# Attention heads worked off in halves of 256 queries, with the next head's projections spread over the head's tiles

## The chip, the cores and the metric

The kernel runs on one core of a Trainium2 chip. A core has five engines with a queue each: TensorE (PE in the profile; its weight loads are listed as PEld), VectorE (DVE), ScalarE (ACT), GpSimd (POOL) and SyncE (SP), which here only issues DMA transfers. Matmul results land in PSUM, in banks of 128 x 512 floats; all else works in SBUF. The metric is the device time of one execution in microseconds (us). It is taken in several runs, and one further execution is recorded by the hardware profiler.

## The reference

Two sequences of 1024 tokens, 256 wide, go through four residual layers, each of them x + f(layernorm(x)), all in float32:

```python
x = x + _L0_attn_ref(_layernorm(x, axis=-1), ...)   # 16 heads of 128, causal, ALiBi
x = x + _L0_ffn_ref(_layernorm(x, axis=-1), ...)    # ternary weights, SiLU-gated, RMS norm
x = x + _L1_attn_ref(_layernorm(x, axis=-1), ...)   # state space (Mamba): conv, scan over tokens
x = x + _L1_ffn_ref(_layernorm(x, axis=-1), ...)    # gated, keeps the two largest of each four
```

The change is in the first of them. A head's share is this, with wq, wk, wv of 256 x 128 and wo of 128 x 256:

```python
q, k, v = xn @ wq, xn @ wk, xn @ wv
s = clip(q @ k.T / sqrt(128), -1024, 1024) + causal_mask + slope[h] * position_of_key
out += softmax(s) @ v @ wo
```

## The kernel before

**Chunks.** The tokens are cut into four chunks of 512: both halves (u = 0 and 1) of the first sequence, then of the second. A chunk goes through all four layers. The kernel writes two streams of work that run beside each other: the attention of chunk k, and `rest(k - 1)`, the three later layers of the chunk before it. Chunk 0's attention has instead the quantization of the ternary weights beside it. The last chunk's `rest(3)` runs alone at the end, with the output projections of chunk 2's last layer held back for it (`held`, `fill_in`).

**One head.** `attention()` (L382) goes over 64 heads, 16 a chunk, and over four tiles of 128 queries in each. For a tile, `scores` (L355) multiplies the tile's queries with all keys up to the tile's end. That is up to 512 keys in chunks with u = 0, and 640 to 1024 with u = 1, in pieces of 512. VectorE takes each piece out of PSUM with the clip and the causal mask (L366), adds the ALiBi row and finds the row's extreme in one pass (L372), and ScalarE takes the exponential and its row sum (L377). `turn` (L286) transposes the tile on TensorE in blocks of 128 and copies the blocks to pT (L296). `values` (L298) multiplies pT with v for all 512 queries of the head, in one PSUM bank, and copies the result to z (L309). `project` (L311) multiplies z with wo, and VectorE scales by the reciprocal of the row sums and adds to x (L324). `qkv` (L328) makes q, k and v of the next head.

**What sets the order.** `attention()` is a generator that yields after each tile. What is to come later stands in the list `later` with a number of tiles to wait. A tile's `turn` comes LAG = 2 tiles after its scores; `values` with the last turn, which is in the next head's tile 1; `project` one tile after that; `qkv` in tile 1. At a chunk's last tile the list is emptied at once. The loops at L970 to L978 draw one tile of attention, and then as many pieces of `rest` as its share of a list of costs (`cost`, L952) says, over the 64 tiles of a chunk. A piece of the state-space loop is one of 64 products: two multiplications on GpSimd (L736, L771), a scan on VectorE (L757), an exponential on ScalarE (L750), and four transposes that add on TensorE (L701). Its rows bs and cs are fetched by SP's queue (L691).

The order written is a priority, not the order issued. The framework's planner estimates when each instruction could start, takes the earliest written of those that can, chooses between VectorE and ScalarE for a copy written as `nc.any`, and fixes each engine's queue. Within a queue the chip keeps that order.

**Buffers that the change touches.** Names with one tag share a fixed number of buffers: pT three (a head with u = 0 holds one, with u = 1 two), z, kT, v and qT two, s four. PSUM has two banks for scores, three (`mm`) that serve pt, z, o and the projections of q, k and v, and three for the rest. `load_head` (L262) fetches the next head's weights and ALiBi row, and in chunks with u = 1 also the kept keys and values of the sequence's first half (L282, L283), which `qkv` stored in DRAM (L350, L352).

## Time and profile before

| | |
|---|---|
| Median of 3 runs | 1837.7 us (1834.47 to 1837.82) |
| Profiled execution, span from first to last instruction | 1836.9 us |
| What lies around that span | the page gives no other time for that execution; the median is 0.8 us above the span |
| TensorE, VectorE, ScalarE, GpSimd busy | 94%, 66%, 52%, 45% of the span |
| Matmul instructions, weight loads | 7956 of each |
| Mean granted TensorE clock | 0.989 |
| Attention of chunks 0, 1, 2, 3 (first L372 to the next chunk's) | 20 to 231, 231 to 735, 735 to 1123, 1123 to 1594 us |
| State-space loops beside chunks 1, 2, 3 | 355 to 566, 830 to 1005, 1244 to 1454 us |
| `rest(3)` alone | from 1594 us on |

In the profile a row names line, engine, operation and tiles as out<-in, then the shape. A matrix product in float32 is two matmul instructions with a weight load each, so that 64 heads with 4 or 8 products of z make 768. A matmul's time has the pipeline's depth in it, and in a stream the next one starts before it ends; the distance between starts is what it costs. A wait names the engine that stood, what it was about to do, and what it waited for.

### The profile page before, as it was taken

To read this page: it belongs to the slowest core of one execution; us is meant where nothing else is said; L and a number is where in the kernel's file an instruction comes from. 1 tells how busy PE (TensorE), PEld (TensorE's weight loads), DVE (VectorE), ACT (ScalarE), POOL (GpSimd) and SP (SyncE) were. 2 spreads that over 40 slices of the span, in tenths; PEclk is the share of its full clock that TensorE was granted. 3 is DMA by queue.
4 is the path that set the end of the run, shared out by engine and by line. 5 is a ranking of instruction groups with operands and counts; after the bars stand their busy time and mean duration, and the time that the engine had idled before them with its cause. 6 is when DMAs were issued, how large, how long until landed. Compare 5 with 4: busy or idle time off the path is not lost. (4 is left out here: it accounts for less than half of the span.)

```text
span 1836.9 us, 24217 instructions
## 1 busy us (share of the span) xinstructions
PE 1718.3 (94%) x7956; PEld 1144.2 (62%) x7956; DVE 1218.3 (66%) x2349; ACT 963.7 (52%) x1789; POOL 832.2 (45%) x674
## 2 busy tenths in 40 slices
PE   7999999998999999998888999999999999998899
PEld 4666666555656557755555667756656565566895
DVE  5666555777785473458886565557788655667975
ACT  3444474656563553555554545566555446446742
POOL 3324032588892000419998000418898500035870
PEclk9999999999999999999999999999999999999999
DMA  6443512466662311337787324227665430212541
GB/s 201 128 142 128 193 46 88 149 203 204 216 202 91 103 52 48 125 109 232 245 247 224 116 71 141 82 67 228 226 214 184 142 115 26 75 53 86 178 136 57
DMA packets 178301, 255.99 MB, mean 139 GB/s; under 512 B 16240, under 2 KB 90992, under 8 KB 177152
## 3 DMA queue, kind: packets, MB, share of 16 engines
q1 hardware_dynamic: 176752, 241.61, 41.4%
q0 software_dynamic: 1152, 12.58, 1.9%
q8 instruction: 63, 1.03, 0.2%
q14 instruction: 62, 0.51, 0.1%
q10 hardware_dynamic: 272, 0.26, 0.0%
HBM read 232.04 MB, written 22.35 MB: 138 GB/s over the span
## 5 line engine op out<-in xcount | busy, mean ns | idle before, releaser
L771 POOL TENSOR_TENSOR hc<-hs,cs 128x512 f32<-128x512 f32 x256 | 362.1, 1428 | 10.8 <-DVE ss L366 3.1
L362 PE MATMUL s<-kT,qT 128*128 128x512 f32 (+3 forms) x768 | 302.7, 495 | 19.9 <-DVE ss L366 18.0
L377 ACT ACTIVATE ss<-ss,nm 128x128 f32<-128x128 f32 (+7 forms) x256 | 198.8, 776 | 183.5 <-DVE nm L372 174.1
L366 DVE SCALAR_TENSOR_TENSOR ss<-s,lower 128x512 f32<-128x512 f32 (+3 forms) x384 | 204.6, 549 | 121.0 <-PE s L362 119.4
L736 POOL TENSOR_TENSOR db<-du,bs 128x512 f32<-128x512 f32 x192 | 259.2, 1356 | 44.4 <-DVE hs L757 30.6
L304 PE MATMUL z<-pT,v 128*128 128x512 f32 (+3 forms) x768 | 264.5, 492 | 10.9 <-ACT pT L296 10.2
L372 DVE CUSTOM_DVE_ANT_0 ss<-ss,alibi 128x128 f32<-128x128 f32 (+7 forms) x256 | 241.3, 945 | 3.5
L750 ACT ACTIVATE da<-dl,a_neg 128x512 f32<-128x512 f32 x256 | 177.9, 698 | 115.6 <-DVE hs L757 90.6
L304 PEld LDWEIGHTS z<-pT,v 128*128 128x128 f32 x768 | 142.8, 190 | 145.1 <-issue 92.7
L296 ACT COPY pT<-pt 128x512 f32<-128x512 f32 (+3 forms) x321 | 145.4, 474 | 162.0 <-PE pt L293 160.4
L293 PE MATMUL pt<-ident,ss 128*128 128x128 f32 x1152 | 180.3, 279 | 32.1 <-DVE x L324 18.5
L293 PEld LDWEIGHTS pt<-ident,ss 128*128 128x128 f32 x1152 | 140.0, 142 | 94.7 <-DVE x L324 33.0
L362 PEld LDWEIGHTS s<-kT,qT 128*128 128x128 f32 x768 | 127.9, 193 | 84.1 <-issue 43.4
L757 DVE TENSOR_TENSOR_SCAN hs<-da,db 128x512 f32<-128x512 f32 x128 | 153.8, 1210 | 38.6 <-ACT da L750 20.8
L757 DVE TENSOR_TENSOR_SCAN hs<-da,carry,db 128x512 f32<-128x512 f32 x128 | 159.1, 1269 | 24.4 <-POOL hc L771 14.7
L324 DVE SCALAR_TENSOR_TENSOR x<-o,rr,x 128x256 f32<-128x256 f32 x256 | 108.9, 476 | 76.7 <-PE o L318 76.5
L701 PE MATMUL y<-ident,hc 128*128 128x128 f32 x1024 | 144.8, 279 | 8.4 <-POOL hc L771 8.4
L342 PEld LDWEIGHTS pv<-wv,xT_a 128*128 128x128 f32 x1024 | 124.4, 192 | 37.1 <-issue 25.3
L342 PE MATMUL pv<-wv,xT_a 128*128 128x128 f32 x1024 | 125.8, 275 | 5.5 <-ACT zs L309 3.4
L701 PEld LDWEIGHTS y<-ident,hc 128*128 128x128 f32 x1024 | 121.0, 145 | 14.3 <-POOL hc L771 11.9
L318 PE MATMUL o<-wo,zs 128*128 128x256 f32 x512 | 125.4, 386 | 4.1 <-ACT kT L338 3.0
L335 PE MATMUL pq<-xT_a,wq 128*128 128x512 f32 x256 | 122.7, 601 | 0.7 <-ACT xT_a L148 0.7
(204 smaller groups left out, 2468.7 us busy)
## 6 DMA issues: line engine op xcount, KB each, us to landing
cs<-bcd SPq DMA_DIRECT2D x256, 256.0 KB, 3.8
bs<-bcd SPq DMA_DIRECT2D x192, 256.0 KB, 4.3
alibi<-alibi_d SPq DMA_DIRECT2D x32, 512.0 KB, 4.2
wq<-in_wqT_dram SPq DMA_DIRECT2D x64, 128.0 KB, 3.5
wk<-in_wkT_dram SPq DMA_DIRECT2D x64, 128.0 KB, 3.1
wv<-in_wvT_dram SPq DMA_DIRECT2D x64, 128.0 KB, 2.8
wo<-in_woT_dram SPq DMA_DIRECT2D x64, 128.0 KB, 2.8
alibi<-alibi_d SPq DMA_DIRECT2D x32, 256.0 KB, 3.6
```

Of the source, the lines that this page charges most:

```text
L293: nc.tensor.transpose(tp[:, i, :], s[:, (kb0 + i) * P : (kb0 + i + 1) * P], ident)
L304: nc.tensor.matmul(zp[:, q0:], lhsT=st["v_all"][:, kb, :], rhs=st["pts"][kb // 4][:, kb % 4, q0:], start=(kb == 0), stop=(kb == last),)
L342: nc.tensor.matmul(vp[:, t, :], lhsT=xT[:, c, t * P : (t + 1) * P], rhs=st["v"][:, c, :], start=(c == 0), stop=(c == KC - 1),)
L362: nc.tensor.matmul(sp[:, :n], lhsT=st["qT"][:, j * P : (j + 1) * P], rhs=st["kT"][:, k0 : k0 + n], start=True, stop=True,)
L366: nc.vector.scalar_tensor_tensor(s[:, k0 : k0 + n], sp[:, :n], CLIP, lower[:, S - W + k0 : S - W + k0 + n], op0=ALU.min, op1=ALU.max,)
L372: pace["tile"] = nc.vector.tensor_tensor_reduce(out=s[:, :W], in0=s[:, :W], in1=st["alibi"][:, :W], scale=1.0, scalar=3.0e38, op0=ALU.add, ...
L377: nc.scalar.activation(s[:, :W], s[:, :W], AF.Exp, bias=nm, scale=-1.0, accum_out=st["rs"][:, j : j + 1])
L701: nc.tensor.matmul(yTs[c][:, t * P : (t + 1) * P], lhsT=h[:, t * P : (t + 1) * P], rhs=ident, is_transpose=True, start=start and t == 0, s ...
L736: nc.gpsimd.tensor_tensor(db[i], du, brow.pop(i), ALU.mult)
L750: nc.scalar.activation(da[i], parts[c][0], AF.Exp, scale=a_neg[:, c, n : n + 1])
L757: nc.vector.tensor_tensor_scan(out=hs[i], data0=da.pop(i), data1=db.pop(i), initial=0.0 if first else carry[:, n, c : c + 1], op0=ALU.mult ...
L771: nc.gpsimd.tensor_tensor(hc[i], hs.pop(i), crow.pop(i), ALU.mult)
```

## The change

A head's last steps are done for 256 queries at a time. `values` and `project` get a number `half`: z of a half goes over the keys up to that half's end, into the left half of a PSUM bank, and its copy, the reciprocal of its row sums and its two additions to x follow from it. z has three buffers of half the size. A half's `values` comes LAG + 1 = 3 tiles after the half's last scores, `project` one tile later. That puts them, for a head's first half, in the next head's tiles 0 and 1, and for the second half in tiles 2 and 3.

`qkv` is cut in three: `queries` in tile 0, `keys` in tile 1 and `new_values` in tile 3. The kept v is fetched in tile 2 (`load_values`), the kept k as before. The next chunk's layernorm is written in tile 2 of the last head but one (before: tile 0 of the last head).

At a chunk's end `later` is no longer emptied: its steps fall in the first four tiles of the next chunk. Only after the very last tile is it worked off, in the order of tiles. So `rest(k - 1)` begins with the chunk's fourth tile, and its costs are spread over 61 tiles.

```diff
--- before.py
+++ after.py
@@ -278,10 +278,13 @@
         w["kT"] = a2.tile([P, S], F32, tag="kT", name=f"kT_{k}_{h}")
         w["v_all"] = a2.tile([P, NT, DH], F32, tag="v", name=f"v_{k}_{h}")
         if u:
-            kd, vd = kept.pop((b, h))
-            nc.sync.dma_start(out=w["kT"][:, :U], in_=kd)
-            nc.sync.dma_start(out=w["v_all"][:, :UT, :], in_=vd)
+            nc.sync.dma_start(out=w["kT"][:, :U], in_=kept.pop(("k", b, h)))
         return w
+
+    def load_values(k, h, w):
+        b, u = CH[k]
+        if u:
+            nc.sync.dma_start(out=w["v_all"][:, :UT, :], in_=kept.pop(("v", b, h)))
 
     def turn(k, h, j, s, st):
 
@@ -295,47 +298,62 @@
                 )
             nc.any.tensor_copy(st["pts"][kb0 // 4][:, 0:n, j * P : (j + 1) * P], tp[:, 0:n, :])
 
-    def values(k, h, st):
+    def values(k, h, half, st):
         u = CH[k][1]
-        zp = ps_z(f"z_{k}_{h}")
-        last = (u + 1) * UT - 1
+        zp = ps_z(f"z_{k}_{h}_{half}")
+        at, W = half * UT // 2, U // 2
+        last = u * UT + at + UT // 2 - 1
         for kb in range(last + 1):
-            q0 = max(0, kb - u * UT) * P
+            q0 = max(0, kb - u * UT - at) * P
             nc.tensor.matmul(
-                zp[:, q0:], lhsT=st["v_all"][:, kb, :],
-                rhs=st["pts"][kb // 4][:, kb % 4, q0:], start=(kb == 0), stop=(kb == last),
+                zp[:, q0:W], lhsT=st["v_all"][:, kb, :],
+                rhs=st["pts"][kb // 4][:, kb % 4, at * P + q0 : at * P + W],
+                start=(kb == 0), stop=(kb == last),
             )
-        st["z"] = a2.tile([P, U], F32, tag="z", name=f"zs_{k}_{h}")
-        nc.any.tensor_copy(st["z"], zp)
-
-    def project(k, h, st):
-
-        rr = a3.tile([P, UT], F32, tag="rr", name=f"rr_{k}_{h}")
-        nc.vector.reciprocal(rr, st["rs"])
-        for t in range(0, UT, 2):
-            op = ps_mm(f"o_{k}_{h}_{t}").rearrange("p (a m) -> p a m", a=2)
-            for i in range(2):
-                ended["by"] = nc.tensor.matmul(
-                    op[:, i, :], lhsT=st["z"][:, (t + i) * P : (t + i + 1) * P], rhs=st["o"],
-                    start=True, stop=True,
-                )
-            for i in range(2):
-                xt = x[k][:, t + i, :]
-                nc.vector.scalar_tensor_tensor(
-                    xt, op[:, i, :], rr[:, t + i : t + i + 1], xt, op0=ALU.mult, op1=ALU.add
-                )
-
-    def qkv(k, h, st, xT):
-        u = CH[k][1]
+        st["z"][half] = a2.tile([P, W], F32, tag="z", name=f"zs_{k}_{h}_{half}", bufs=3)
+        nc.any.tensor_copy(st["z"][half], zp[:, :W])
+
+    def project(k, h, half, st):
+
+        at = half * UT // 2
+        rr = a3.tile([P, UT // 2], F32, tag="rr", name=f"rr_{k}_{h}_{half}")
+        nc.vector.reciprocal(rr, st["rs"][:, at : at + UT // 2])
+        op = ps_mm(f"o_{k}_{h}_{half}").rearrange("p (a m) -> p a m", a=2)
+        for i in range(2):
+            ended["by"] = nc.tensor.matmul(
+                op[:, i, :], lhsT=st["z"][half][:, i * P : (i + 1) * P], rhs=st["o"],
+                start=True, stop=True,
+            )
+        for i in range(2):
+            xt = x[k][:, at + i, :]
+            nc.vector.scalar_tensor_tensor(
+                xt, op[:, i, :], rr[:, i : i + 1], xt, op0=ALU.mult, op1=ALU.add
+            )
+
+    def turned_input(n, k, h, st, xT):
+        pp = ps_mm(f"p{n}_{k}_{h}")
+        for c in range(KC):
+            nc.tensor.matmul(
+                pp, lhsT=st[n][:, c, :], rhs=xT[:, c, :], start=(c == 0), stop=(c == KC - 1)
+            )
+        return pp
+
+    def queries(k, h, st, xT):
         st["qT"] = a2.tile([P, U], F32, tag="qT", name=f"qT_{k}_{h}")
+        nc.scalar.activation(
+            st["qT"], turned_input("q", k, h, st, xT), AF.Copy, scale=-1.0 / math.sqrt(DH)
+        )
+
+    def keys(k, h, st, xT):
+        b, u = CH[k]
         kT = st["kT"][:, u * U : (u + 1) * U]
-        for n, dst, scale in (("q", st["qT"], -1.0 / math.sqrt(DH)), ("k", kT, 1.0)):
-            pp = ps_mm(f"p{n}_{k}_{h}")
-            for c in range(KC):
-                nc.tensor.matmul(
-                    pp, lhsT=st[n][:, c, :], rhs=xT[:, c, :], start=(c == 0), stop=(c == KC - 1)
-                )
-            nc.scalar.activation(dst, pp, AF.Copy, scale=scale)
+        nc.scalar.activation(kT, turned_input("k", k, h, st, xT), AF.Copy, scale=1.0)
+        if u < NU - 1:
+            kept["k", b, h] = dr.tile([P, U], F32, tag="kd", name=f"kd_{k}_{h}", bufs=H)
+            nc.sync.dma_start(out=kept["k", b, h], in_=kT)
+
+    def new_values(k, h, st, xT):
+        b, u = CH[k]
         vp = ps_mm(f"pv_{k}_{h}").rearrange("p (t m) -> p t m", t=UT)
         for t in range(UT):
             for c in range(KC):
@@ -346,11 +364,8 @@
         v = st["v_all"][:, u * UT : (u + 1) * UT, :]
         nc.any.tensor_copy(v, vp)
         if u < NU - 1:
-            kd = dr.tile([P, U], F32, tag="kd", name=f"kd_{k}_{h}", bufs=H)
-            nc.sync.dma_start(out=kd, in_=kT)
-            vd = dr.tile([P, UT, DH], F32, tag="vd", name=f"vd_{k}_{h}", bufs=H)
-            nc.sync.dma_start(out=vd, in_=v)
-            kept[CH[k][0], h] = kd, vd
+            kept["v", b, h] = dr.tile([P, UT, DH], F32, tag="vd", name=f"vd_{k}_{h}", bufs=H)
+            nc.sync.dma_start(out=kept["v", b, h], in_=v)
 
     def scores(k, h, j, st):
 
@@ -385,38 +400,45 @@
         live = [load_head(0, 0)]
         for k in range(1, len(CH)):
             load_x(k)
-        qkv(0, 0, live[0], xns[0])
+        for f in (queries, keys, new_values):
+            f(0, 0, live[0], xns[0])
         later = []
         for i, (k, h) in enumerate(heads):
             st = live.pop(0)
-            if i + 1 < len(heads):
-                live.append(load_head(*heads[i + 1]))
+            ahead = heads[i + 1] if i + 1 < len(heads) else None
+            if ahead:
+                live.append(load_head(*ahead))
             u = CH[k][1]
             st["pts"] = [
                 a3.tile([P, 4, U], F32, tag="pT", name=f"pT_{k}_{h}_{i}") for i in range(u + 1)
             ]
             st["rs"] = a3.tile([P, UT], F32, tag="rs", name=f"rs_{k}_{h}")
+            st["z"] = {}
             for j in range(UT):
                 s = scores(k, h, j, st)
                 later.append((LAG, lambda a=(k, h, j, s, st): turn(*a)))
-                if j == UT - 1:
-                    later.append((LAG, lambda a=(k, h, st): values(*a)))
-                    later.append((LAG + 1, lambda a=(k, h, st): project(*a)))
-                if j == UT - 1 and h == H - 1:
-                    for _, f in later:
-                        f()
-                    later = []
-                else:
-                    now = [f for n, f in later if n == 0]
-                    later = [(n - 1, f) for n, f in later if n]
-                    for f in now:
-                        f()
-                if j == 1 and i + 1 < len(heads):
-                    qkv(*heads[i + 1], live[0], xns[heads[i + 1][0]])
-                if j == 0 and h == H - 1 and k + 1 < len(CH):
+                if j % 2:
+                    later.append((LAG + 1, lambda a=(k, h, j // 2, st): values(*a)))
+                    later.append((LAG + 2, lambda a=(k, h, j // 2, st): project(*a)))
+                now = [f for n, f in later if n == 0]
+                later = [(n - 1, f) for n, f in later if n]
+                for f in now:
+                    f()
+                if ahead:
+                    if j == UT // 2:
+                        load_values(*ahead, live[0])
+                    make = {0: queries, 1: keys, UT - 1: new_values}.get(j)
+                    if make:
+                        make(*ahead, live[0], xns[ahead[0]])
+                if j == UT // 2 and h == H - 2 and k + 1 < len(CH):
 
                     with tc.issue_after(tiles[-UT].ins) if k == 0 else nullcontext():
                         normed(k + 1)
+                if not ahead and j == UT - 1:
+                    while later:
+                        for f in [f for n, f in later if n == 0]:
+                            f()
+                        later = [(n - 1, f) for n, f in later if n]
                 yield k
 
 
@@ -971,8 +993,10 @@
         r, done = rest(k - 1), 0.0
         for i in range(H * UT):
             next(heads)
+            if i < UT - 1:
+                continue
             whole = cost(k - 1)
-            while done < whole * (i + 1) / (H * UT):
+            while done < whole * (i + 2 - UT) / (H * UT + 1 - UT):
                 done += next(r, whole)
         for _ in r:
             pass
```

## The prediction

> **What bounds the kernel now.** I read the page's first part, then stretches of the span cut where the state-space loop begins and ends, then TensorE's waits, then one head's matmuls in order of time, then the end of the last head.
>
> ```profile
> PE 1718.3 (94%) x7956; PEld 1144.2 (62%) x7956; DVE 1218.3 (66%) x2349; ACT 963.7 (52%) x1789; POOL 832.2 (45%) x674
> ```
>
> TensorE (PE) is the bound on average, but its busy time counts pipeline latency, so stages must be seen one by one (columns: PE, weight loads, DVE, ACT, POOL busy us, clock, DMA):
>
> ```profile
> 20.00:231.00 211.00, 204.91 (x968) 135.58 (x968) 139.88 (x390) 101.85 (x255) 58.33 (x51) 1.00 0.46 149
> 355.00:566.00 211.00, 192.63 (x941) 127.44 (x940) 170.12 (x298) 122.72 (x223) 184.68 (x132) 1.00 0.66 207
> 830.00:1005.00 175.00, 141.91 (x709) 101.13 (x710) 143.53 (x209) 93.09 (x194) 169.24 (x130) 0.93 0.78 240
> 1244.00:1454.00 210.00, 192.45 (x942) 127.53 (x941) 168.80 (x301) 122.99 (x223) 184.93 (x132) 1.00 0.65 209
> ```
>
> The first is chunk 0's attention, the others the state-space loops beside the attention of chunks 1, 2 and 3. In chunk 2 GpSimd (POOL) sets the pace: 169 of 175 us. In chunks 1 and 3 PE leaves 18 us of 211 and POOL 26.
>
> ```profile
> PE pt L293 <- DVE x L324: 18.5, 16, 2.4
> PE s L362 <- DVE ss L366: 18.0, 21, 1.3
> PE z L304 <- ACT pT L296: 10.2, 13, 1.7
> ...
> PE pt L293 <- ACT ss L377: 6.0, 8, 2.0
> ```
>
> These are the attention's own waits (us in total, times, longest). Their cause is in the order of one head of chunk 1:
>
> ```profile
> 426.95 5.86 PE L304 MATMUL z<-pT,v 128*128 128x512 f32 x16
> 432.64 1.88 PE L335 MATMUL pq<-xT_a,wq 128*128 128x512 f32 x4
> 434.36 1.88 PE L335 MATMUL pk<-xT_a,wk 128*128 128x512 f32 x4
> 436.08 1.95 PE L342 MATMUL pv<-wv,xT_a 128*128 128x128 f32 x16
> ...
> 439.37 1.89 PE L318 MATMUL o<-wo,zs 128*128 128x256 f32 x8
> 441.10 0.60 PE L293 MATMUL pt<-ident,ss 128*128 128x128 f32 x4
> ...
> 445.05 0.33 PE L293 MATMUL pt<-ident,ss 128*128 128x128 f32 x1 [1.62 <-DVE x L324]
> ...
> 451.74 1.56 PE L362 MATMUL s<-kT,qT 128*128 128x512 f32 x4 [1.25 <-DVE ss L366]
> ```
>
> From 426.95 to 437.86 PE does values and projections alone; no score is made, and VectorE (DVE) gets no tile. Then scores and transposes come faster than DVE empties their banks, and PE waits.
>
> **Spacings.** Starts a row apart divided by the count give what an instruction costs in a stream: 128x512 0.430 us (432.64 to 434.36, four), 128x256 0.216 (439.37 to 441.10, eight), projected values 0.111 (1.78 in 16), transposes 0.109 (same chunk: eight from 453.14 to 454.01); a 384-wide one I take as 0.323, between them. By these a head of chunks 1 and 3 costs PE 21.0 us: before, its four tiles take 1.8, 13.0, 3.8 and 2.4 us; after, 6.0, 4.8, 5.3 and 5.0. A head of chunks 0 and 2 costs 12.3 (2.2 scores, 2.2 z, 1.1 transposes, 1.7 o, 3.4 q and k, 1.8 v), 3.1 a tile.
>
> **Halved values: +1.** z has 768 instructions; halves make 32 x 6 x 2 + 32 x 14 x 2 = 1280, with 512 more weight loads. The columns are the same (1280 and 3328 a head): 10 x 0.430 + 2 x (0.323 + 0.216 + 0.109) = 5.60 us before, 24 x 0.216 + 4 x 0.109 = 5.62 after, under 1 us over 32 heads. The bound on the other side is every added load in the open: the row of z's loads has 190 ns, 512 x 0.190 = 97 us. I take the low end, because L318 is just such a stream, 256 wide with a load each, and runs at 0.216.
>
> The Trainium skill speaks against this edit: "TensorE: Matmul & The Clock Gate", section "The mechanism", lets a load overlap a running matmul only where the row groups differ, and its section "LDWEIGHTS (loading the stationary operand)" prices 128 columns at 128/1.2 = 107 ns. All loads here use all rows, so by that rule the 512 would add 55 us and the sum below would be about 1870. The trace disagrees: o's eight matmuls and eight loads fit in 1.73 us.
>
> **Twice as many small steps: +1.** 64 more reciprocals of 168 ns are 10.8 us of DVE. z's evictions become 128 of about 373 ns (the row of pT at 128x256 on ScalarE, ACT) for 64 of 581: 10.6 us more. ACT is 52% busy, and outside the two loops DVE idles; in the loops DVE is 170 of 211 and PE waits on it, 8 heads x 168 ns, 1.3 us each. I take 1; without cover it is 21.
>
> **Projections and values spread: -23.** The waits that uneven tiles make, by stretch: 8.5 (s on ss), 5.2 (pt on x), 2.2 (z on pT), 1.0 (pv on zs) in chunk 1's loop; 7.8, 4.9, 2.2, 1.0 in chunk 3's; 3.4 (pt on the exponential), 1.2, 0.7 in chunk 0: 38 us. Chunk 2's are left out, since POOL sets its pace. I take 60%: a loop that lost all its waits would take 194 us, not far from POOL's own work, 64 x 2 x 1.27 + 12 x 1.27 = 178, and two engines that near to each other's time still stop each other now and then. Ends: 38 gained, or nothing; below nothing is a rival. What is late next is POOL.
>
> **The rest starts three tiles later: +5.** L972's loop spreads the former chunk's later layers over 61 tiles, not 64. The state-space loop has 2.2 x 69 = 152 of 303 cost units in chunk 2, so it lies beside 30.6 tiles, not 32.1. It still takes POOL's 175 us, and 1.5 tiles x 3.1 us of attention fall outside: +4.6. In chunks 1 and 3 PE is the nearer bound and the same move costs nothing unless POOL takes over.
>
> **Chunks run on into each other: 0, and -5 at the end.** At the three inner boundaries PE's order already mixes the old chunk's values with the next scores; its waits there are at most 0.8 us each. After the last head nothing covers:
>
> ```profile
> 1596.55 1.09 PE L293 MATMUL pt<-ident,ss 128*128 128x128 f32 x8 [2.00 <-ACT ss L377]
> ...
> 1597.88 5.86 PE L304 MATMUL z<-pT,v 128*128 128x512 f32 x16 [0.24 <-ACT pT L296]
> ...
> 1604.41 1.99 PE L318 MATMUL o<-wo,zs 128*128 128x256 f32 x8 [0.68 <-ACT zs L309]
> 1605.58 1.74 DVE L324 SCALAR_TENSOR_TENSOR x<-o,rr,x 128x256 f32<-128x256 f32 x4 [7.21 <-PE o L318]
> ```
>
> Only the second half needs the last tile: 14 x 0.216 + 2 x 0.109 = 3.2 us of z, not 5.7 (-2.4), two x additions, not four (-0.9), and the first pair of layernorm tiles is out of the way (its xn starts 1.6 ahead of the second's, -1.6). The first half fills the 2.0 us of wait. Ends -2.4 and -7.
>
> **Moved at no cost.** The load of kept v (32 of them) goes two tiles later on SP's queue, and still waits there for the old buffer's last reader (SP stood 183.6 us, 18 times, at L283 for z). Behind it wait the bs and cs rows and the next weights. It lands in 3.6 us and is read over four tiles later. Without that cover POOL waits: all waits on bs make 13.8 us now. The stores of k and v are as many as before. Layernorm of the next chunk goes two tiles ahead, as does its first reader.
>
> **Sum.** 1836.9 (the profiled span) + 1 + 1 - 23 + 4.6 - 5 = 1815.5. The median of the runs shown is 0.8 above that span; so 1816.
>
> **Rivals.** *POOL takes the loops over* (chance 0.15). With 61 tiles the loops of chunks 1 and 3 hold 1.5 x 5.25 = 8 us less of PE's work, and PE's gain there is eaten: chunk 0 gives 3 and the end 5, against 7 of cost: 1836. For it: POOL 185 of 211. Against: its own work is 178, the rest its waits on DVE's scans (13.6 and 17.1 us).
>
> *A new wait at the second half of z* (0.25, slower). In chunks 1 and 3 a head holds two of the three pT buffers. The whole z was done 8 us before the next head's first transposes (432.6 to 441.1); its second half now stands in the same tile, just ahead of them. If the copy of the last pT is late there, PE stops, with scores, projections and the state space's transposes queued behind it, and ACT waits for a buffer. Such waits are there now: 13, mean 0.8, longest 1.7. One in each of 32 heads at 1.2 us is 38: 1854. It decides from 22 / 32 = 0.7 us a head. Against: the copy has a tile of 5 us to be done in.
>
> *Nothing spreads* (0.05). The order written is not the order issued: at 745 us z matmuls stand between layernorm's transposes. If the planner makes the same lumps, the sum without the 23 is 1839.
>
> My forecast has 0.55, with 1795 to 1832 as its own range. The range 1792 to 1850 leaves out a tenth on each side: a gain beyond all 38 of the waits, and the dearer half of the second rival. 0.2% (3.7 us) is about what a measurement of this kernel can tell from no change. Faster: 0.54 from the forecast, 0.06 and 0.02 from the first and third rivals; same 0.09; slower 0.25 and a few hundredths from the others.
>
> **What would show it.** Right: z x1280 with o's spacing of 0.216 kept; waits of s on ss and pt on x under half; chunk 1's and 3's loops near 200 us, chunk 2's still 175; the end of attention about 5 us shorter. Wrong: z's loads in the open, z's wait on pT at 32 times, or the loops still at 211 with POOL over 195.

## The result, and the profile after

The changed kernel takes 1857.3 us (median of 4 runs, 1855.36 to 1863.3) against 1837.8 in runs beside it: 1.0122 times the time, 95% interval 1.0102 to 1.0143. It is slower by 20 us, where 21 us less were forecast.

The profiled execution is the longest of the four (1863.3 us; its span is 1861.4), 6 us over the median. Busy time of the engines, whole span:

```profile
PE 1735.5 (93%) x8468; PEld 1249.4 (67%) x8468; DVE 1308.0 (70%) x2552; ACT 947.3 (51%) x1736; POOL 821.3 (44%) x674
```

The 512 added matmuls and loads are there. VectorE (DVE) is busy 90 us longer, ScalarE (ACT) 16 less: the planner put 72 of the 128 copies of z on DVE (12 of 64 before), and 137 copies of pT (63 before).

Busy time in stretches, as in the prediction (columns: window, length, PE, weight loads, DVE, ACT, POOL with counts, granted clock, DMA share, GB/s): chunk 0's attention, and the state-space loops beside chunks 1, 2 and 3.

```profile
20.00:220.00 200.00, 199.84 (x1031) 146.56 (x1030) 158.85 (x427) 98.17 (x254) 57.18 (x51) 1.00 0.48 156
360.00:580.00 220.00, 196.89 (x988) 145.17 (x987) 182.90 (x326) 109.07 (x195) 182.31 (x133) 0.94 0.62 195
847.00:1025.00 178.00, 139.02 (x710) 99.57 (x709) 150.77 (x221) 90.24 (x186) 167.16 (x130) 0.92 0.75 228
1275.00:1495.00 220.00, 197.37 (x988) 144.88 (x987) 182.02 (x326) 109.11 (x194) 182.34 (x133) 0.94 0.61 194
```

Chunk 0 has become 11 us shorter, and TensorE (PE) is busy in 199.8 of its 200 us. The loops take 220, 178 and 220 us, for 211, 175 and 210. POOL has a little less to do in them (182.3 us, for 184.7) and stands longer. The clock, 1.00 in loops 1 and 3 before, is 0.94.

PE's waits, whole span (us in total, times, longest):

```profile
PE pq L336 <- DVE zs L314: 25.5, 10, 4.4
PE y L723 <- POOL hc L793: 23.5, 22, 2.1
PE o L323 <- DVE zs L314: 10.5, 7, 2.4
...
PE z L308 <- ACT pT L299: 3.0, 3, 2.3
PE pt L296 <- DVE x L329: 2.7, 2, 1.7
PE s L377 <- DVE ss L381: 2.0, 2, 1.0
```

The waits that were to go are gone: s on ss 18.0 to 2.0 us, pt on x 18.5 to 2.7, z on pT 10.2 to 3.0. New ones stand first: the products pq and o now wait for z's copy, 43.6 us in all with two smaller rows. For o the copy is its input; q's projection needs a PSUM bank of the `mm` set, of which z holds one until it is copied.

**Where the time went.** I cut both traces at the reduction of each chunk's first tile of scores (L372 before, L387 after), at that of the very last tile, and at the first and last of a loop's 64 multiplications hc. PE's *work* in a part is its matmuls times the spacing of their width (0.430, 0.216, 0.109 us; about half of it for the ternary layer's products, of which 512-wide ones start 0.23 us apart at 1638 us after). *Idle* is the rest, so it holds PE's waits and also what a halved clock costs.

| Part | before | after | difference |
|---|---|---|---|
| up to the first tile | 19.5 | 20.3 | +0.8 |
| chunk 0 (idle in it) | 211.7 (14.5) | 199.4 (2.7) | -12.3 |
| chunks 1 to 3, outside the loops: duration (work, idle) | 766.3 (730.7, 35.5) | 784.2 (752.5, 31.7) | +17.9 |
| the three loops: duration (work, idle) | 596.5 (496.4, 100.2) | 617.5 (475.3, 142.2) | +20.9 |
| after the last tile | 242.9 | 240.0 | -2.9 |
| sum | 1836.9 | 1861.4 | +24.5 |

What is lost is PE's idle time in the loops, 42 us more, and it has two parts: the loops are 21 us longer, and 21 us of PE's work that lay in them now lies outside. The loops of chunks 1 and 3 hold 28 tiles of attention, for 31. In loop 1 PE's waits sum to 23 us, 18 before, and its halved clock costs up to 13.7, nothing before. By chunk the attention of chunks 1, 2 and 3 takes 6, 15 and 18 us longer.

**How a loop stands.** Three queues, each kept in order, wait on each other. In loop 1 (what each engine waited for; after, then before):

```profile
POOL db L758 <- DVE hs L779: 22.4, 3, 8.4
POOL hc L793 <- PE y L723: 9.1, 4, 4.1
DVE ss L381 <- PE s L377: 25.6, 10, 5.9
```

```profile
POOL db L736 <- DVE hs L757: 13.6, 3, 5.9
DVE v L347 <- PE pv L342: 15.9, 2, 8.0
DVE hs L757 <- ACT da L750: 10.4, 4, 9.4
DVE ss L366 <- PE s L362: 8.9, 11, 3.3
```

All of DVE's waits there sum to 34 us after and 41 before, so DVE does not stand longer, but elsewhere in its queue. POOL's sum to 37 and 26.

And one of after's three stands in order of time, from PE's, DVE's and POOL's timelines (start, us, idle before it in brackets):

```profile
414.86 0.87 DVE L387 CUSTOM_DVE_ANT_0 ss<-ss,alibi 128x640 f32<-128x640 f32 x1
...
420.32 1.02 DVE L381 SCALAR_TENSOR_TENSOR ss<-s,lower 128x512 f32<-128x512 f32 x2 [3.79 <-PE s L377]
421.38 1.79 DVE L387 CUSTOM_DVE_ANT_0 ss<-ss,alibi 128x768 f32<-128x768 f32 x1
...
426.23 0.69 DVE L381 SCALAR_TENSOR_TENSOR ss<-s,lower 128x512 f32<-128x512 f32 x1 [1.59 <-PE s L377]
...
427.90 1.21 DVE L779 TENSOR_TENSOR_SCAN hs<-da,db 128x512 f32<-128x512 f32 x1
```

```profile
418.63 3.72 POOL L793 TENSOR_TENSOR hc<-hs,cs 128x512 f32<-128x512 f32 x3 [0.55 <-PE y L723]
429.19 2.05 POOL L758 TENSOR_TENSOR db<-du,bs 128x512 f32<-128x512 f32 x1 [6.83 <-DVE hs L779]
```

From 413.8 to 427.9 DVE's queue holds no scan. It stands twice there for scores that PE makes late. POOL runs out of scans, needs the next one to free a buffer of db, and stands 6.83 us. PE in turn lacks POOL's products: its wait of y on hc, second in its list above, was 8.4 us before. The longest stretch without a scan in loops 1 and 3 is 10.1 us before and 16.1 after.

### The profile page after: what moved, and what is told of

Read it like the earlier page. It is cut to its first block, busy times and chain, and to the rows that moved or that the text cites. A ratio compares the mean times of both kernels' runs of the same rounds, so it can differ in the third digit from the quotient of the medians.

```text
span 1861.4 us, 25366 instructions
## 1 busy us (share of the span) xinstructions
PE 1735.5 (93%) x8468; PEld 1249.4 (67%) x8468; DVE 1308.0 (70%) x2552; ACT 947.3 (51%) x1736; POOL 821.3 (44%) x674
## 4 chain that ended last, share of the span: by engine, by line
PE 63%; DVE 11%; POOL 10%; issue 6%; DMA 5%; ACT 4%; SPq 1%; POOLq 0%; DVEq 0%; ACTq 0%
PE s L377 9%; PE z L308 8%; PE pq L336 5%; POOL hc L793 5%; PE pk L336 5%; PE pt L296 4%; PE o L323 4%; DVE hs L779 4%; PE pv L360 4%; POOL db L758 3%; PE g_g L463 3%; PE in L630 3%; PE u_g L463 3%; DMA cs<-bcd 3%; PE y L723 2%
## 5 line engine op out<-in xcount | busy, mean ns | idle before, releaser
L793 POOL TENSOR_TENSOR hc<-hs,cs 128x512 f32<-128x512 f32 x256 | 343.4, 1360 | 30.9 <-PE y L723 20.4
L758 POOL TENSOR_TENSOR db<-du,bs 128x512 f32<-128x512 f32 x192 | 267.1, 1400 | 67.2 <-DVE hs L779 44.8
L308 PE MATMUL z<-pT,v 128*128 128x256 f32 (+1 forms) x1280 | 274.0, 360 | 3.2 <-ACT pT L299 3.0
L308 PEld LDWEIGHTS z<-pT,v 128*128 128x128 f32 x1280 | 238.6, 191 | 49.3 <-ACT pT L299 4.9
L387 DVE CUSTOM_DVE_ANT_0 ss<-ss,alibi 128x128 f32<-128x128 f32 (+7 forms) x256 | 256.9, 1003 | 5.4
L299 ACT COPY pT<-pt 128x512 f32<-128x512 f32 (+3 forms) x247 | 115.8, 486 | 161.7 <-PE pt L296 160.7
L296 PE MATMUL pt<-ident,ss 128*128 128x128 f32 x1152 | 170.9, 275 | 2.7 <-DVE x L329 2.7
L336 PE MATMUL pq<-xT_a,wq 128*128 128x512 f32 x256 | 135.8, 654 | 31.9 <-DVE zs L314 25.5
L323 PE MATMUL o<-wo,zs 128*128 128x256 f32 x512 | 135.6, 385 | 13.3 <-DVE zs L314 10.5
L336 PE MATMUL pk<-xT_a,wk 128*128 128x512 f32 x256 | 127.1, 620 | 7.9 <-ACT qT L343 4.0
```

Source lines behind the costliest of these rows:

```text
L296: nc.tensor.transpose(tp[:, i, :], s[:, (kb0 + i) * P : (kb0 + i + 1) * P], ident)
L308: nc.tensor.matmul(zp[:, q0:W], lhsT=st["v_all"][:, kb, :], rhs=st["pts"][kb // 4][:, kb % 4, at * P + q0 : at * P + W], start=(kb == 0), ...
L323: ended["by"] = nc.tensor.matmul(op[:, i, :], lhsT=st["z"][half][:, i * P : (i + 1) * P], rhs=st["o"], start=True, stop=True,)
L336: nc.tensor.matmul(pp, lhsT=st[n][:, c, :], rhs=xT[:, c, :], start=(c == 0), stop=(c == KC - 1))
L387: pace["tile"] = nc.vector.tensor_tensor_reduce(out=s[:, :W], in0=s[:, :W], in1=st["alibi"][:, :W], scale=1.0, scalar=3.0e38, op0=ALU.add, ...
L758: nc.gpsimd.tensor_tensor(db[i], du, brow.pop(i), ALU.mult)
```

## The experiments

The recorded expectations number the theories in the order in which they came up. Those that matter: copies of z on VectorE hold PSUM banks, TensorE stands for them and its clock falls (1); the rest, crowded into 61 tiles, makes GpSimd the pace (2); the spread itself is at fault (3); GpSimd and the scans pace the loops, so late scans become lost time (4); the order that the planner writes is a draw, which any change of the program redraws (7); the even order is worse in itself (8).

### e1: is it the clock, or z's copies on VectorE?

```diff
-        nc.any.tensor_copy(st["z"][half], zp[:, :W])
+        nc.scalar.copy(st["z"][half], zp[:, :W])
```

> The changed kernel with one edit: the copy of z is tied to ScalarE. Theory 1 (the copies of the halves that fell to VectorE, 72 of 128, stand behind scans and hold a PSUM bank that the next query projection needs; TensorE stands up to 4.4 us there and its clock then falls): the waits of pq and o on zs (43.6 us now) fall under 10, the granted clock in the state-space loops of chunks 1 and 3 goes from 0.94 to 0.98 or more, these loops from 220 to about 205 us, and the time from 1857 to 1822 to 1835. Theory 2 (the rest of the former chunk, crowded into 61 tiles, makes GpSimd the pace): the loops stay at 215 or more, the waits move to another releaser, and the time stays over 1848.

Measured: 1864.0 us, 1.0148 (1.0122 to 1.0173). The loops, and the largest of PE's waits:

```profile
362.00:582.00 220.00, 192.18 (x989) 139.52 (x988) 179.72 (x315) 110.76 (x205) 183.47 (x133) 0.98 0.63 195
...
1278.00:1497.00 219.00, 192.08 (x986) 140.26 (x985) 179.27 (x315) 111.06 (x205) 181.77 (x132) 0.97 0.63 194
```

```profile
PE pq L336 <- ACT zs L314: 37.3, 14, 5.2
...
PE o L323 <- ACT zs L314: 6.3, 9, 1.2
```

The clock is back at 0.98 and 0.97 and the loops last as long as with 0.94: losing less clock did not shorten them. The waits for z's copy did not fall: they are 43.6 us as before the edit, now all on ACT. So the part of theory 1 that blames VectorE and the clock falls, but what these waits cost is not tested here. e4 below bears on it: it has no wait of pq on zs, and its loops are as long in sum.

### e2, e3, e4: the parts of the change one by one

e2: the changed kernel, with the list worked off at each chunk's last tile and the rest spread over 64 tiles again.

```diff
-                if not ahead and j == UT - 1:
+                if h == H - 1 and j == UT - 1:
...
-            if i < UT - 1:
-                continue
             whole = cost(k - 1)
-            while done < whole * (i + 2 - UT) / (H * UT + 1 - UT):
+            while done < whole * (i + 1) / (H * UT):
```

> The changed kernel without its last part: the list of later steps is worked off at each chunk's last tile, and the rest is spread over 64 tiles again. Theory 2 (61 tiles): the loops of chunks 1 and 3 go back to 31 tiles and about 211 us, chunk 2's outside part loses its 5 us, and the time falls to 1835 to 1843. Theory 1 (copies of z on VectorE): the waits on zs and the low clock in the loops stay, and the time stays at 1850 to 1860.

e3: the kernel before, with chunks that run on and the rest from the third tile.

```diff
-                if j == UT - 1 and h == H - 1:
...
+                if j == UT - 1 and i + 1 == len(heads):
...
+            if i < LAG:
+                continue
             whole = cost(k - 1)
-            while done < whole * (i + 1) / (H * UT):
+            while done < whole * (i + 1 - LAG) / (H * UT - LAG):
```

> The kernel before with the run-on alone: the list of later steps is not worked off at a chunk's end, and the rest begins with the chunk's third tile and is spread over 62. Theory 2: slower, 1843 to 1850, with the loops of chunks 1 and 3 over fewer than 31 tiles and POOL waiting no more. Theory 1: chunk 2 loses 3 to 5 us outside its loop as forecast, the loops of chunks 1 and 3 stay near 211 us at full clock, and the time is 1836 to 1842.

e4: the kernel before, with q, k and v of the next head made in tiles 0, 1 and 3 (and the next chunk's layernorm where the change has it).

```diff
...
-                if j == 1 and i + 1 < len(heads):
-                    qkv(*heads[i + 1], live[0], xns[heads[i + 1][0]])
+                if i + 1 < len(heads):
+                    make = {0: queries, 1: keys, UT - 1: new_values}.get(j)
+                    if make:
+                        make(*heads[i + 1], live[0], xns[heads[i + 1][0]])
...
```

> The kernel before with the spread of the projections alone: queries in tile 0, keys in tile 1, values in tile 3, z whole. Theory 1 (halved z on VectorE is the cause): no wait of pq on zs comes up, the waits of s on ss and pt on x fall by half, and the time is 1822 to 1835. Theory 3 (the spread itself is at fault: a projection in each tile asks for one of the three shared PSUM banks while they wait for copies): new waits of pq, pk or pv of 20 us or more, clock below 0.98 in the loops, and 1845 to 1855.

Measured: e2 1849.6 us, 1.0059 (1.0035 to 1.0083); e3 1886.9, 1.0273 (1.0255 to 1.0290); e4 1853.0, 1.0086 (1.0067 to 1.0105). Spread alone costs 14 us, run-on alone 48, halves with spread 11, and all three together 20: the parts do not add. e2 lies between the ranges of its two theories and e3 above both of its own; e4 lies in theory 3's range, but without the new waits of projections that theory 3 asked for. By part of the span:

| Kernel | chunk 0 | three loops | PE's work in them | idle in them |
|---|---|---|---|---|
| before | 211.7 | 596.5 | 496.4 | 100.2 |
| e4, spread alone | 203.3 | 618.8 | 497.7 | 121.2 |
| e2, without run-on | 201.6 | 627.8 | 496.2 | 131.6 |
| e3, run-on alone | 211.1 | 601.8 | 467.4 | 134.4 |
| after | 199.4 | 617.5 | 475.3 | 142.2 |

Chunk 0, which has no scans beside it, gains 8 us from the spread and a few more from the halves. In e4 PE's wait of s on ss is gone (18.0 us before), but pt on x stays at 17.2 us and z on pT grows from 10.2 to 27.4: the spread alone moves waits more than it ends them. Its loops of 218, 183 and 218 us come with DVE busy 169.0 us in the first, 170.1 before. In the loops, length does not follow work: e3 has 29 us less work in them than before, and they are 5 us longer.

```profile
376.00:585.00 209.00, 184.64 (x883) 121.93 (x881) 168.55 (x292) 112.61 (x205) 180.93 (x132) 0.98 0.65 206
```

That is e3's first loop: 29 tiles in the time in which the kernel before has 31.

### e5, e6, e9: GpSimd's load

Beside attention the multiplication by cs on GpSimd is left out (192 of its 256 instructions), so the layer's values are wrong by that factor; the scan's results go to the transposes directly, with the buffers of both. e5 is so changed from before, e6 from after, e9 from e2.

```diff
...
+                if not tail_end:
+                    hc[i] = hs.pop(i)
+                    return
                 hc[i] = part("hc", f"hc_{k}_{c}_{n}", 5 + more)
...
```

> The kernel before with the multiplication of each scanned row by its cs row left out beside the attention (256 - 64 = 192 GpSimd multiplications fewer, the scanned rows are added as they are, in the buffers of both; the output is not the reference's). It halves GpSimd's work in the loops of chunks 1 to 3. Theory 4 (the loops are paced by GpSimd and by the scans on VectorE, and TensorE's evenness buys nothing there): the loops of chunks 1 and 3 go from 211 to 195 to 200 us, chunk 2's from 175 to about 140, and the time falls by 50 to 65 us. Theory 1 or 3 (TensorE's own waits for copies of PSUM banks pace the loops): the loops of chunks 1 and 3 stay over 205 and only chunk 2's falls.

> The changed kernel with the same multiplications left out, in the same buffers (the output is not the reference's). Theory 4: with GpSimd out of the way the loops follow TensorE, where the changed kernel has 28 tiles to 31; it is level with or faster than the kernel before without the multiplications, by 0 to 20 us, and not 19 slower. Theories 1 and 3: the waits of pq on zs stay, and it stays 15 us or more slower than its counterpart.

> Halves and spread without the run-on, and without the 192 GpSimd multiplications by the cs rows (the output is not the reference's). To be set beside the kernel before without them (1800.8 us) and the changed kernel without them (1804.2). Theory 4 (the loops' loss is GpSimd's stands): here halves and spread show what they are worth to TensorE alone: chunk 0 -10, end -3, loops no longer than the kernel before has them: 1780 to 1790. Theories 1 and 3 (banks and copies): the loops of chunks 1 and 3 stay 5 to 10 us longer than the 205 of the kernel before without them, 1800 to 1808.

Measured: e5 1800.8 us, 0.9809 (0.9791 to 0.9826); e6 1804.2, 0.9828 (0.9809 to 0.9847); e9 1819.2, 0.9888 (0.9873 to 0.9902). First loop of e5, then of e6, from the first scan to the last, since no hc is left to cut at:

```profile
350.00:555.00 205.00, 195.76 (x959) 129.83 (x957) 163.05 (x302) 123.73 (x225) 101.46 (x72) 1.00 0.70 218
```

```profile
356.00:549.00 193.00, 180.79 (x951) 135.43 (x950) 166.88 (x318) 107.76 (x191) 95.96 (x72) 0.98 0.72 226
```

With half of GpSimd's work gone the changed kernel's disadvantage falls from 20 us to 3. From the first transpose of y to the last, loop 1 takes 214 us in e5 and 212 in e6, where it is 224 before and 232 after. (By scans alone the changed kernel's loop is the shorter one with GpSimd's work whole too, 211 us for 215.) But theory 4 misses its figures: e5 gains 35 us, for 50 to 65, and e9, the same design without the run-on, is 18 us slower than e5 (15 by the ratios), where it was to be faster. GpSimd's load may be a part of it and is not the whole. Each of these kernels is one order, and e13 to e16 show how far one order can lie from another.

### e7 and e10: buffers, and the stretch without scans

```diff
-                    db[i] = part("db", f"db_{k}_{c}_{n}", 4)
+                    db[i] = part("db", f"db_{k}_{c}_{n}", 5)
```

> The changed kernel with five buffers for db in place of four (more does not fit). Theory 4, with the stop passed on through VectorE's queue (a scan stands behind scores that TensorE makes late, and GpSimd, four products ahead at most, stands with it up to 8 us): a product more of lead takes 2.5 us off each of the some ten stands, the waits of db on hs go from 45 to under 30 us and the time falls by 5 to 12 us. Theories 1 and 3: no change beyond 4 us.

e10, also from after: a scan of the state space is tied to come after the reduction of an earlier tile of scores, here of one two tiles older. In the order that results, more tiles of scores stand between two scans where the channel changes.

```diff
-        pace["front"] = tiles[-2] if len(tiles) >= 2 else None
+        pace["front"] = tiles[-4] if len(tiles) >= 4 else None
```

> The changed kernel with the scans let go four tiles behind the scores in place of two: the planner then puts three tiles' scores, not two, between two scans on VectorE's queue at each change of channel. If the stretch of VectorE's queue without a scan (14 to 17 us there, 11 in the kernel before) is what makes GpSimd stand 7 to 8 us each time, the loops of chunks 1 and 3 grow by some 5 us for each of three changes, 230 us or more, and the time to 1870 or more. If the stretch is harmless: no change beyond 4 us.

Measured: e7 1859.7 us, 1.0133 (1.0113 to 1.0153): nothing. POOL's waits on scans for db (22.4 us in loop 1) become waits at hc: the four largest there, all at hc, sum to 32 us, where the three largest after, at db and hc, sum to 35. e10 1884.7 us, 1.0245 (1.0230 to 1.0260); its first loop:

```profile
361.00:592.00 231.00, 198.34 (x988) 143.98 (x987) 178.47 (x324) 110.10 (x196) 180.46 (x133) 0.95 0.61 186
```

The same work of every engine takes 231 us for 220, with stretches of up to 20.6 us without a scan. This came out as expected if such stretches cost time in loops 1 and 3, but it is one order, and other runs speak against it as a rule. e13 below has stretches of 17.3 to 18.6 us without a scan at all three changes of channel, and its loops 1 and 3 take 212 us with 30 tiles in them and 25 us of idle time of PE each, as before.

### e11 and e12: less work beside the loops

In both the gate of the state-space layer (transposes, product) is left out beside attention, and its input to the output projection is wrong there. e11 is made from after, e12 from before.

```diff
                 nc.scalar.copy(ysb, yTs.pop(c))
+                if not tail_end:
+                    return
```

> The changed kernel without the gate at a channel's end beside the attention (four transposes of the sum and its product with sz are left out, 12 times; the output is not the reference's). If the stands at the changes of channel make the loops long: the loops of chunks 1 and 3 fall from 220 to 205 us or less and the time by 20 to 40 us. If they come from the copies and banks of the attention: the time falls by the 12 transposes and products alone, under 10 us.

> The kernel before without the same gates (the output is not the reference's). It too stands three times a loop, 5.9, 5.9 and 1.8 us: the loops of chunks 1 and 3 fall from 211 to about 200 us and the time by 15 to 25 us; the gap to the changed kernel without gates is then under 10 us, where it is 19 with them. If the gap stays at 15 or more, the change of channel is not where the two differ.

Measured: e11 1854.4 us, 1.0087 (1.0070 to 1.0104); e12 1862.5, 1.0127 (1.0111 to 1.0142). Leaving work out made the kernel *before* 23 us slower than itself, where 15 to 25 us less were expected. e11 is only 3 us below after's time (6 by the ratios), with loops 1 and 3 of 216 and 215 us: the gate at the changes of channel is not what makes them long. e12's loops, and POOL's first wait in loop 1:

```profile
355.00:576.00 221.00, 194.59 (x944) 129.72 (x944) 168.71 (x302) 123.70 (x226) 184.36 (x133) 0.99 0.65 199
839.00:1019.00 180.00, 143.91 (x696) 100.69 (x697) 142.31 (x202) 95.03 (x196) 166.80 (x130) 0.91 0.75 233
1256.00:1478.00 222.00, 196.35 (x942) 130.38 (x942) 167.80 (x301) 123.60 (x225) 184.25 (x133) 0.98 0.63 198
```

```profile
POOL db L736 <- DVE hs L757: 22.8, 3, 9.7
```

These are the changed kernel's lengths (loops 220, 178, 220; POOL 22.4 us on scans) without any of the change, though with 32 tiles in loops 1 and 3, not 28. DVE is busy 168.7 us in the first, so its added work isn't needed for that length. The kernel before looks like one good order among others.

### e13 to e16: the same two designs, redrawn

The rest is drawn half a tile earlier or later; nothing else differs. Before (e13, e14), then after (e15, e16; here the later one of each pair):

```diff
-            while done < whole * (i + 1) / (H * UT):
+            while done < whole * (i + 1 + -0.5) / (H * UT):
```

```diff
-            while done < whole * (i + 2 - UT) / (H * UT + 1 - UT):
+            while done < whole * (i + 2 - UT + -0.5) / (H * UT + 1 - UT):
```

> The kernel before with the rest of the former chunk drawn half a tile earlier against the attention, nothing else. Theory 7 (the planner's order in the loops is a draw, and the kernel before has a good one): its loops go to 214 to 222, 177 to 185 and 214 to 222 us and the time to 1845 to 1865. Theory 8 (the even order is worse in itself): within 5 us of 1838.

> The kernel before with the rest drawn half a tile later. Theory 7: 1845 to 1865, loops longer as in the run half a tile ahead, but not by the same. Theory 8: within 5 us of 1838.

> The changed kernel with the rest drawn half a tile earlier. Theory 7: anywhere from 1835 to 1870, with loops of 205 to 225 us, and the mean of the changed kernel's draws within 8 us of the mean of the other's. Theory 8: within 5 us of 1857, loops of chunks 1 and 3 at 217 to 222.

> The changed kernel with the rest drawn half a tile later. Theory 7: anywhere from 1835 to 1870. Theory 8: within 5 us of 1857.

| Kernel | time | ratio to before | loops | work in them | idle in them |
|---|---|---|---|---|---|
| before | 1837.1 | 1 | 596.5 | 496.4 | 100.2 |
| e13, half a tile ahead | 1861.0 | 1.0121 (1.0099 to 1.0144) | 602.8 | 493.5 | 109.4 |
| e14, half a tile behind | 1881.1 | 1.0237 (1.0219 to 1.0255) | 608.3 | 476.8 | 131.5 |
| after | 1857.3 | 1.0122 (1.0102 to 1.0143) | 617.5 | 475.3 | 142.2 |
| e15, after, half ahead | 1854.7 | 1.0088 (1.0066 to 1.0109) | 598.8 | 470.9 | 127.7 |
| e16, after, half behind | 1863.9 | 1.0143 (1.0122 to 1.0164) | 616.2 | 476.5 | 139.7 |

Three draws of the kernel before give 1837, 1861 and 1881 us, mean 1860; three of the changed one 1857, 1855 and 1864, mean 1859. Half a tile moves the old design by more than the change does, and its one order that was kept is the best of the three. e15's loops of 209, 181 and 208 us come with stretches of 16.3 us without a scan, so no single number of an order that I looked at tells its length. Theory 8's figure of 1838 fails in e13 and e14. Theory 7 holds for the times of e13, e15 and e16; e14 lies above its range of 1845 to 1865, and e13's loops 1 and 3 of 212 us lie under the 214 to 222 expected.

The two redrawn orders of before do not lose their time where the change does. Of the idle time of PE that e13 adds in chunks 1 to 3, 9 us lie in the loops, all in chunk 2's, and 13 outside them; of e14's, 31 and 8. The change adds 42 in the loops and takes 4 off outside. In the loops alone the three orders of before have 100, 109 and 132 us of idle time, the three of the change 142, 128 and 140.

### e17 and e18: the late start of the rest

With GpSimd's work whole, the three loops take 597 to 628 us in all runs above but e10, whether 494 to 498 or 467 to 477 us of PE's work lie in them. If so, the work that the late start moves out of them is lost. Here the whole change is kept, but at the fourth tile the rest catches up with the old due times; e18 is half a tile ahead of e17.

```diff
             if i < UT - 1:
                 continue
             whole = cost(k - 1)
-            while done < whole * (i + 2 - UT) / (H * UT + 1 - UT):
+            while done < whole * (i + 1) / (H * UT):
```

> The changed kernel, but the rest keeps the due times of the kernel before: still nothing in a chunk's first three tiles, then it makes up for them at the fourth tile, so that its costs are spread over 64 tiles and not 61. Over the runs so far the three state-space loops together take 610 us (597 to 628) in five kernels whose rest is due from the first tile on and 610 us (599 to 618) in five whose rest starts three tiles late, although TensorE's own work inside them is 494 to 498 us in the first (477 where the rest is drawn half a tile late) and 467 to 477 in the others. Theory: a loop's length is a draw of the order written, and does not follow the work that lies in it, so that the late start costs the 20 us that it moves out of the loops. Then here TensorE's work in the loops is back at 494 to 498 us, the loops take 597 to 628 together, chunks 1 to 3 take 1227 of work plus 33 of waits outside plus the loops less that work, 1361 to 1393, and the kernel 1821 to 1853, 1837 in the middle. Rival: the order with spread projections costs what it costs in chunks 1 to 3 wherever the rest begins (the three phases of the changed kernel gave 1855, 1857 and 1864): then 1853 to 1866, with loops that are longer by as much work as has come into them.

> The same, with the rest drawn half a tile earlier: a second draw of the same design, since one draw tells little where a half-tile shift has moved the kernel before by 24 us. Theory of work moved out of the loops: again 494 to 498 us of TensorE's work in the loops and 1821 to 1853; the two runs differ by the length of their loops. Rival: 1853 to 1866 again.

Measured: e17 1850.6 us, 1.0078 (1.0057 to 1.0098), loops 627.3 with 496.5 of work; e18 1845.4, 1.0044 (1.0028 to 1.0060), loops 606.5 with 481.5. e17's loops:

```profile
348.00:570.00 222.00, 200.00 (x1033) 147.18 (x1032) 181.25 (x324) 113.90 (x209) 181.65 (x132) 0.98 0.64 197
835.00:1019.00 184.00, 141.96 (x722) 103.83 (x723) 149.40 (x223) 91.78 (x192) 166.20 (x130) 0.92 0.77 226
1258.00:1479.00 221.00, 201.29 (x1037) 149.09 (x1038) 181.08 (x329) 115.03 (x210) 182.00 (x133) 0.98 0.63 198
```

Both fall in the theory's range, at its dear end, and below all three draws of the late start: mean 1848 against 1859. So by the means the late start costs some 11 us, half of the 20 that I expected. In e17 21 us of work came back into the loops and they grew by 10; in e18 the work did not come back to 494, which was expected of it and is a miss. PE's idle time in loops 1 and 3 is 32 to 35 us each in both, for 41 after; in chunk 2's loop it is 62 and 60, for 60. But e15, which starts late, has 32 and 31 in loops 1 and 3. With two draws against three that differ by 5 to 9 us among themselves, 11 is a rough number, and that it is the late start's is not shown.

### e8: what can be kept

Halves and spread projections in chunk 0 and halves in the very last head; in chunks 1 to 3 the order of before, without run-on.

```diff
...
-                if j % 2:
+                by_halves = k == 0 or (k == len(CH) - 1 and h == H - 1)
+                if by_halves and j % 2:
                     later.append((LAG + 1, lambda a=(k, h, j // 2, st): values(*a)))
                     later.append((LAG + 2, lambda a=(k, h, j // 2, st): project(*a)))
+                if not by_halves and j == UT - 1:
+                    later.append((LAG, lambda a=(k, h, st): whole_values(*a)))
+                    later.append((LAG + 1, lambda a=(k, h, st): whole_project(*a)))
...
+                    spread = {0: [queries], 1: [keys], UT - 1: [new_values]}
+                    for make in (spread if k == 0 else {1: [queries, keys, new_values]}).get(j, []):
...
```

> A kernel of both: halves and spread projections where no state space runs beside the attention (chunk 0, and halves in the very last head), the order of the kernel before in chunks 1 to 3, no run-on. Every theory that puts the loss into the state-space loops: chunk 0 takes 200 to 203 us in place of 212, the loops stay at 211, 175 and 211, the end gains 2 to 4 us, and the time is 1822 to 1828. If the planner's order in the loops is upset by what precedes them, they lengthen by 5 to 10 us each and the time is 1840 or more.

Measured: 1824.7 us (1821.39 to 1826.02), 0.9935 (0.9917 to 0.9954): faster than both kernels.

```profile
20.00:221.00 201.00, 200.84 (x1038) 147.52 (x1037) 158.84 (x427) 98.68 (x254) 57.21 (x51) 1.00 0.49 157
345.00:555.00 210.00, 192.49 (x942) 127.54 (x941) 169.04 (x308) 122.90 (x223) 184.91 (x132) 1.00 0.69 208
823.00:998.00 175.00, 140.46 (x709) 99.94 (x710) 143.27 (x218) 92.44 (x193) 169.40 (x130) 0.94 0.79 240
1236.00:1446.00 210.00, 192.51 (x940) 127.34 (x939) 169.05 (x305) 122.62 (x223) 184.84 (x132) 1.00 0.66 208
```

Chunk 0 has the changed kernel's gain (201.7 us for 211.7), what follows the last tile takes 238.1 for 242.9, and the loops are those of before to within 1.3 us, the good draw kept. Time, chunk 0 and loops are as expected; the end gained 4.8 us, for 2 to 4.

## Why the prediction was wrong

**"Projections and values spread: -23" is the step that failed.** It took PE's waits in the loops as time that goes when their cause goes, with the rest of the order staying as it was. The waits did go (over the whole span s on ss, pt on x and z on pT from 47 us to 8). The loops did not shorten: 617.5 us for 596.5, with PE waiting for z's copy and DVE for scores instead. e4, the spread of the projections alone, costs 14 us, with loops 22 us longer. The step left out that a change of program gives three engines another order: half a tile's shift, without any of the change, costs 24 and 44 us (e13, e14). No term of the sum and no rival had it. That the change's own loss is such a bad draw is argued from this and not shown: e13 and e14 lose 9 and 31 us of PE's time in the loops, the change 42. In chunk 0, where no scans run beside the attention, the same step was right and too small: some 10 us (e2 and e8, without the run-on) in place of the 60% of 5.3.

**"The rest starts three tiles later: +5" was mis-sized.** It counted chunk 2 alone, where POOL sets the loop's length, and took the loops of chunks 1 and 3 to get shorter with fewer tiles. Chunk 2's loop kept its length nearly (178 us for 175, with 29 tiles for 30), but PE's idle time in it grew from 50 to 60 us. That is not the late start's: e13 and e17 have 59 and 62. Loops 1 and 3 held 28 tiles for 31 and were 8 and 9 us longer. With the old due times put back (e17, e18) the kernel is about 11 us faster, and what shows of it lies in loops 1 and 3, where the prediction took the move to be free. With so few draws, that this is the late start's price is not shown.

**"Halved values: +1" held.** The second half of a head with u = 1 is 14 matmuls 256 wide and 2 of 128:

```profile
398.92 3.54 PEld L308 LDWEIGHTS z<-pT,v 128*128 128x128 f32 x16
399.24 3.41 PE L308 MATMUL z<-pT,v 128*128 128x256 f32 x16
...
402.48 0.71 PE L296 MATMUL pt<-ident,ss 128*128 128x128 f32 x5
```

From 399.24 to 402.48 is 3.24 us, and 14 x 0.216 + 2 x 0.109 = 3.24: none of the 16 loads adds to the spacing. The rule of the Trainium skill that was weighed against it ("TensorE: Matmul & The Clock Gate", "The mechanism": a load overlaps a running matmul only where the row groups differ) does not fit these rows. The same section also lets a load go ahead into a background weight buffer, and with that they agree. The 55 us of the rule did not come.

**"Twice as many small steps: +1" named the right risk and priced it low.** DVE's work grew by 90 us, not by 21, since the planner moved copies to it; in loop 1 it is busy 182.9 us, for 170.1. e1 took the z copies off it again, but DVE stayed busy 179.7 us there. e4 and e12 speak against it: their first loops take 218 and 221 us with DVE busy 169.0 and 168.7, so a loop gets that long without this work.

**"0, and -5 at the end" was right in sign.** What follows the last tile took 2.9 us less. The last head's second half of x begins 6.5 us after its last transposes (1633.17 for 1626.69), where all of x began 9.0 after them; the expected wait of 2.0 us at those transposes is gone.

**Moved at no cost** held for the kept v: POOL has no wait on bs among its first in loop 1 (4.8 us before).

**The rivals.** *A new wait at the second half of z* did not come: 3 waits, 3.0 us. The new wait stands at z's copy, one step later in the same chain: 43.6 us of pq and o. e4's loops of 218, 183 and 218 us come with no wait of pq on z's copy, so it is not needed for their length. *POOL takes the loops over* has the right place: loops 1 and 3 do not shrink with the tiles in them. Its condition, POOL busy above 195, did not come (182): POOL stands 37 us of loop 1, most of it for scans and for y, where it stood 26. *Nothing spreads* is out, the projections stand in separate tiles. The range, up to 1850, lacked the draw: the six kernels of e13 to e16's table spread over 44 us. The measured 1857 lies 7 us above its end; that the second rival's figure of 1854 is near it is luck, since its wait did not come.

**What stays open.** In chunks 1 to 3 the changed kernel is 39 us slower than before. Before's three draws average 20 us more than the one that was kept, and the late start costs about 11. The remaining 8 us are less than the draws scatter, so whether the spread and the halves help or harm beside the state space isn't settled. The idle time in the loops alone, 100 to 132 us in before's draws and 128 to 142 in the change's, leaves room for harm. What in an order makes a good draw isn't either.

## What to carry to other kernels

Where several engines' queues are fixed by a planner and stand near balance, treat the order as a draw (half a tile moved this kernel by 24 and 44 us): before an edit is credited or blamed, shift the due times by a fraction of a step in both kernels, and see how far the time moves without any edit. Waits of an engine in such a stretch are not a sum that can be collected; they are where the slack shows, and it comes back at another instruction. Take an even order where one engine works alone (chunk 0, the last head), and leave a good order standing where three are coupled.

## What the runs showed of the hardware

The granted clock of PE falls to 0.5 for 3.4 or 6.8 us, 22 times after and 9 times before within the span. In 16 of the 22 PE's records have a gap of 2.2 to 4.4 us that starts 2 to 4 us before the fall; in six of these the fall comes before the gap's end. Two gaps of 2.2 and 2.5 us have no fall behind them. One fall is from 385.9 to 392.8 us, around this wait in PE's timeline:

```profile
388.15 3.78 PE L336 MATMUL pq<-xT_a,wq 128*128 128x512 f32 x4 [4.33 <-DVE zs L314]
```

Four matmuls of 512 take 3.57 us to the next start there, where the prediction's rows had 1.72. That the falls did not set the length of the loops is what e1, one order, shows: it has 5.1 and 6.8 us of clock lost in loops 1 and 3 (half the time at 0.5) for 13.7 and 13.7, and its loops are as long.

The Trainium skill, "TensorE: Matmul & The Clock Gate", section "Why this matters for your kernels", warns of gaps of PE above some 3 us between bursts, since a window without work halves the clock. The trace agrees in kind and has shorter gaps ahead of falls. As a price of this change the rule misleads here: 7 to 9 us less of lost clock in a loop left its length as it was.
